# A conditioned two-MLP block: first slots counted on their own, conditioning bias by a matmul, late load of the last weights

## Chip, core and metric

The kernel runs on one core of a Trainium2 chip (trn2). The metric is the device time of one execution in microseconds (us), median of the runs. Engines are named as the profile names them: PE is TensorE (PEld its weight loads), DVE is VectorE, ACT is ScalarE, POOL is GpSimd, SP is SyncE, which here only issues transfers.

## What is computed

`x` is 32 sequences of 128 tokens with 512 features, `t` one conditioning vector of 512 per sequence, `mask` marks some tokens at the end of each sequence (up to 32 of 128). All is float32.

```python
emb = silu(t) @ ada_w + ada_b
shift, scale, gate_msa = split(emb, 3, axis=1)
norm = where(m, layernorm(x) * (1 + scale[:, None]) + shift[:, None], 0)
fwd = gelu(norm @ ssm_w1 + ssm_b1) @ ssm_w2 + ssm_b2
bwd = flip(gelu(flip(norm) @ bwd_w1 + bwd_b1) @ bwd_w2 + bwd_b2)
x = x + gate_msa[:, None] * where(m, fwd + bwd, 0)
ff_ada = silu(t) @ ffada_w + ffada_b
shift_mlp, scale_mlp, gate_mlp = split(ff_ada, 3, axis=1)
ff_norm = layernorm(x) * (1 + scale_mlp[:, None]) + shift_mlp[:, None]
return x + gate_mlp[:, None] * (gelu(ff_norm @ ff_w1 + ff_b1) @ ff_w2 + ff_b2)
```

The first MLP (both directions together, 512 to 1024 to 512) touches only the marked tokens. The second MLP (512 to 1024 to 512) touches all 4096.

## The kernel before

**Slots.** The marked tokens are packed into 512 slots, in four tiles of 128. Which token stands in a slot is counted on the chip. `pick_slots(h)` (L246) compares 256 slot numbers with the first and last slot of each sequence; `slots_to_count` (L254) multiplies the result with the running count of marked tokens, one small matmul for each tile of slots; `counted` (L261) turns that into token numbers on VectorE (compare, sum, add). The opening counts tiles 0 and 1 together (L567), and `gather` (L280) fetches their rows by two indirect transfers on POOL's queue. If more than 512 tokens are marked, a loop at the end (L1557) does the rest; with these inputs it has nothing to do.

**Transfers.** SP issues nearly all loads and stores, in the order of the program. `load_behind_gathers` (L138) writes one element of the destination on POOL first; so the load on SP waits until POOL has come past the gathers, and everything behind it on SP waits too. Each DMA counts up one of eight semaphores in turn, so an issue can also wait for a much older transfer.

**Conditioning.** `modulation_matmuls` (L299) forms `silu(t) @ ada_w` in four column strips of 32 batches, so that partition 32 j + b of `pm` holds block j of batch b. The bias is loaded for all 128 partitions (`load_conditioning_bias`, L129: three transfers of 64 KB for each of the two conditionings) and added by VectorE (`modulation_rows`, L311). `of_slots` (L315) spreads the rows to the slots ("strips"). Between the four groups of L609, and once behind the strips (L617), `keep_clock` (L596) runs matmuls whose result nobody reads, and `on_zeros` (L444) does the same on zeros.

**First MLP.** Tiles 0 and 1 are normalised, transposed (L192), multiplied with `w1` (L649, L201) and `w2` (`project`, L217), and finished by `finish_slots` (L362). Tiles 2 and 3 follow; `finish_late` (L1364) finishes them. Output banks of tiles 0, 1 and 2 begin with the bias (`seeded_with_bias`, L234); that of tile 3 gets it by an addition on VectorE (L1367).

**Second MLP.** It runs over four pairs (`p`) of two sides with four sequences each. Both of its products are made from seven block products, P1 to P7, in the manner of Strassen and Winograd. `FirstProduct` (L1003) does so on two levels: seven streams j, each with P1 to P7, in `window`s (L1185) of seven block products that end stream `old` and begin stream `new` (order 1, 2, 5, 6, 3, 7, 4). Streams 5, 6, 7 and 4 use sums of weights that were stored in DRAM (`t_rows`, L717) and are loaded for each pair by `load_weights` (L1037): block 1 for stream 5, 2 for 6, 3 for 7 (issued when stream 5 has ended, L1426), 4 for 4. `SecondProduct` (L1204) uses `fw2` and the three differences that `Weights.combine` (L383) makes of it: the first two stand in the opening (L1378), the others in the second product of the first pair. `token_sums` (L1015) and `TokenBlocks` (L946) make the sums of the token side on VectorE. `take_first_half` (L861) fetches the result rows of the first MLP into the tiles of a pair, by eight indirect transfers on POOL.

The order on each engine is written out by hand (the program is under a manual schedule until L1546): `fills` and `fill` hang steps behind a given product of a window or step.

Of the kernel before, what the change touches and what calls it, by code (L numbers as in the profile page):

```python
# [9 lines left out]
F32 = mybir.dt.float32  # L10
I32 = mybir.dt.int32
U8 = mybir.dt.uint8
BF16 = mybir.dt.bfloat16
AF = mybir.ActivationFunctionType
ALU = mybir.AluOpType
# [7 lines left out]
def kernel(  # L23
# [105 lines left out]
    def load_conditioning_bias(t, vec, kinds, queue):  # L129

        rows = vec.rearrange("(m j c) -> m j c", m=3, c=P)
        for m in kinds:
            queue.dma_start(t[:, m], rows[m].unsqueeze(1).to_broadcast([KC, B, P]))

# [7 lines left out]
    modb_a = adap.tile([P, 3, P], F32, tag="modb", name="modb_a", bufs=1)  # L142
# [8 lines left out]
    load_conditioning_bias(modb_a, ada_b, range(2), nc.sync)  # L151
# [94 lines left out]
    def pick_slots(h):  # L246

        part = ts(h, NH)
        nc.vector.tensor_scalar(inside[:, part], slot_row[:, part], behind, None, ALU.is_lt)
        nc.vector.scalar_tensor_tensor(  # L250
            pick[:, part], slot_row[:, part], first, inside[:, part], ALU.is_ge, ALU.mult
        )

    def slots_to_count(picked, n, name, bank):  # L254

        pl = bank[0].tile([P, 512], F32, tag=bank[1], name=f"pl_{name}")
        for c in range(n):
            nc.tensor.matmul(pl[:, ts(c, S)], picked[:B, ts(c, P)], rank, start=True, stop=True)
        return pl[:, : n * S].rearrange("p (c s) -> p c s", s=S)
# [38 lines left out]

    def modulation_matmuls(pm, ada, lo, hi, blocks):  # L299
        kinds = ada.rearrange("p k (m d) -> p k m d", d=D)  # L300
        for k in blocks:
            for j in range(KC):
                nc.tensor.matmul(
                    pm[ts(j, B), : (hi - lo) * P],
                    sT[:, k, :],
                    kinds[:, k, lo:hi, ts(j, P)],
                    start=(k == 0),
                    stop=(k == KC - 1),
                )

    def modulation_rows(pm, mod, modb, lo, hi):  # L311
        view = pm[:, : (hi - lo) * P].rearrange("p (m c) -> p m c", c=P)
        nc.vector.tensor_tensor(mod[:, lo:hi], view, modb[:, lo:hi], ALU.add)
# [130 lines left out]
    def on_zeros(*widths):  # L444
        for n in widths:
            nc.tensor.matmul(pm_keep_clock[:, :n], zeros[:, :P], zeros[:, :n], start=True, stop=True)
# [85 lines left out]
    pick_slots(0)  # L532

    nc.vector.tensor_scalar(rank[:, : S - 1], pg[:B, : S - 1], first[:B], None, ALU.add)

# [8 lines left out]
    on_zeros(256)  # L544
    nc.scalar.copy(sT.rearrange("p k b -> p (k b)"), ptr[:, : KC * B])
    warm = stp.tile([1, 1], F32, tag="warm", name="warm", bufs=1)
# [6 lines left out]
    load_conditioning_bias(modb_a, ada_b, (2,), nc.scalar)  # L553

    every = adap.tile([B, 3, P], BF16, name="every")
    nc.vector.memset(every, 1.0)
    for j, batches in ((1, 2 * G), (2, G)):
        nc.gpsimd.affine_select(
            out=every[:, j],
            in_=every[:, j],  # L560
            compare_op=ALU.is_gt,
            fill=0.0,
            base=batches,
            pattern=[[0, P]],
            channel_multiplier=-1,
        )
    token_i = tokens_of(pick[:, :NH], slot_col[:, : NC // 2], NC // 2, "s0", ssm)  # L567
    both = xp.tile([P, 2, D], F32, tag="x", name="xc_0")
    xc += [both[:, c] for c in range(2)]
    gather(xc[0], token_i[:, 0:1])  # L570
    load_behind_gathers(w1[:, :, :D], ssm_w1)
    gather(xc[1], token_i[:, 1:2])
# [15 lines left out]
    pick_slots(1)  # L588
# [4 lines left out]
    nc.vector.tensor_scalar(slot_of, slot_of, FAR, None, ALU.add)  # L593

# [13 lines left out]
    for k in range(KC):  # L608
        modulation_matmuls(pm, ada_a, 0, 2, (k,))  # L609
        if k < KC - 1:  # L610
            keep_clock(1, k)
    slots_of_late = slots_to_count(pick[:, NH:], NC // 2, "s1", (ps_h, "h"))
    nc.vector.tensor_scalar(modb_a[:, 1], modb_a[:, 1], 1.0, None, ALU.add)
    modulation_rows(pm, mod1, modb_a, 0, 2)

    strips = of_slots(pick, (0, 1), mod1, slice(0, 2), 3 * [(ps_o, "o")] + [(ps_h, "h")], "part_s0")
    keep_clock(1, 0)  # L617
# [26 lines left out]
    modb_f = adap.tile([P, 3, P], F32, tag="modb", name="modb_f", bufs=1)  # L644
    load_conditioning_bias(modb_f, ffada_b, range(3), nc.gpsimd)
# [31 lines left out]
    modulation_rows(pm, mod1, modb_a, 2, 3)  # L677
# [45 lines left out]
    for j in range(3):  # L723
        nc.tensor.matmul(pt[:, j : j + 1], every[:, j], count, start=True, stop=True)
# [33 lines left out]
    for n in range(2):  # L758
        own_statistics(raw[n], 2, f"x_{n}")
# [5 lines left out]
    for c in range(2):  # L765
        xn_late.append(
            modulated_by_strips(
                xc[2 + c], strips, c, spare[1][:, c], mv_t[:, c, 0:1], rstd_t[:, c : c + 1]
            )
        )  # L770
        if c == 0:
            nc.vector.tensor_tensor(b2, b2, b2b, ALU.add)
    h1 += hidden(xT_s, NH, w1, 0, AF.Gelu, "s0", ssm, range(KC, HC))
# [8 lines left out]
    store_rows = [finish_slots(0, project(0, h1, w2, "s0", seeded=po_s[0]), gs[0])]  # L782
    own_statistics(raw[3], 2, "x_3")
# [4 lines left out]
    nc.vector.tensor_scalar(modb_f[:, 1], modb_f[:, 1], 1.0, None, ALU.add)  # L788
# [22 lines left out]
    modulation_matmuls(pm, ada_f, 0, 3, range(KC))  # L811

# [19 lines left out]
    normalised_of_side_0(range(1))  # L832
    modulation_rows(pm, mod2, modb_f, 0, 3)
    normalised_of_side_0(range(1, 2))
# [510 lines left out]
    def load_of_pair_1():  # L1345
        nc.sync.dma_start(b2_row, b2[0:1, :])
        broadcast_rows(fb2, ff_b2, nc.sync)
        x_of[1] = [load_side(1, 0, spare), None]
# [7 lines left out]
        6: [turn_rows(3), lambda: load_behind_gathers(fw2, ff_w2), lambda: store_weight_sums(4, 1, 2)] + store_rows,  # L1356
        7: [load_of_pair_1],
# [6 lines left out]
    def finish_late(at, po, bias=None):  # L1364
        t = tp.tile([P, D], F32, tag="t", name=f"t_s_{at}")
        if bias is not None:
            nc.vector.tensor_tensor(t, po, bias, ALU.add)  # L1367
            po = t
        nc.vector.tensor_tensor(t, po, gs[at], ALU.mult)
        nc.vector.tensor_tensor(t, t, xc[at], ALU.add)  # L1370
        nc.sync.dma_start(x1_rows[ts(at, P), :], t)

    finish_late(2, project(0, h1, w2, "s2", {2 * k: turn(k) for k in range(KC)}, seeded=po_s[2]))
    po = project(1, h1, w2, "s3", bank=(ps_h, "h"))
# [3 lines left out]
    fw2_of.combine(0, 1)  # L1378
    for j in (3, 4):
        of_x[0].one(j)  # L1380
    finish_late(3, po, b2)
# [3 lines left out]
    now = FirstProduct(0, of_x[0].cut(), of_w)  # L1385
    now.load_weights(1)
    x_of[1][1] = load_side(1, 1)
    now.load_weights(2)
    for n in range(2):
        now.token_sums(1, n)  # L1390
# [6 lines left out]
    now.seed(2)  # L1397
    now.do(1, "P3")
# [3 lines left out]
    take_first_half(1, x_of[1])  # L1402
    for n in range(2, 4):
        now.token_sums(1, n)
# [5 lines left out]
    for p in range(NP):  # L1410
# [18 lines left out]
        if p == 0:  # L1429
            put(  # L1430
                5, 1, nc.vector.tensor_tensor,
                fb2_step, fb2[:, D // 2 :], fb2[:, : D // 2], ALU.subtract,
            )
        put(6, 0, now.late_gelu, "11")
# [233 lines left out]
```

## Time and profile before

| what | value |
|---|---|
| median of 3 runs (lowest, highest) | 457.67 us (457.63, 458.54) |
| the profiled execution | 457.94 us, of which its span is 456.2 us |
| PE busy in the span | 445.3 us |
| DVE, ACT, POOL busy | 332.8, 176.9, 161.2 us |
| transfers | 70.98 MB, mean 156 GB/s |
| `fw2` load: issued, landed | 70.44, 81.67 us |
| first gather: issued, landed after | 7.95 us, 4.6 us |

How to read the lines: in the timeline a line begins with the start and the busy time of a group in us, then the engine, the line of the kernel, the operation, its output and inputs by tile name, the shape and the count; what stands in brackets is the idle time of the engine just before and what ended it. A float32 matmul of the program is two entries of the trace. In a group line ("| busy, mean ns |") the mean is that of one entry. A line of windows gives the stretch, its length, the busy time (and instructions) of PE, PEld, DVE, ACT and POOL, the granted clock, the share of the DMA engines and the GB/s. Waits for several semaphores are put down to the one that came last.

### The profile page before, as it was taken

To read this page: it belongs to the slowest core of one execution; us is meant where nothing else is said; L and a number is where in the kernel's file an instruction comes from. 1 tells how busy PE (TensorE), PEld (TensorE's weight loads), DVE (VectorE), ACT (ScalarE), POOL (GpSimd) and SP (SyncE) were. 2 spreads that over 40 slices of the span, in tenths; PEclk is the share of its full clock that TensorE was granted. 3 is DMA by queue.
4 is the path that set the end of the run, shared out by engine and by line. 5 is a ranking of instruction groups with operands and counts; after the bars stand their busy time and mean duration, and the time that the engine had idled before them with its cause. 6 is when DMAs were issued, how large, how long until landed. Compare 5 with 4: busy or idle time off the path is not lost.

```text
span 456.2 us, 6196 instructions
## 1 busy us (share of the span) xinstructions
PE 445.3 (98%) x2161; PEld 370.9 (81%) x2161; DVE 332.8 (73%) x570; ACT 176.9 (39%) x387; POOL 161.2 (35%) x155
## 2 busy tenths in 40 slices
PE   8999999979999999999999999999999999999995
PEld 4784485668888888888888888888888888888884
DVE  4797887978779749895796398867963995534645
ACT  3123126244543551545435515454355154552000
POOL 4230560079770000697700006977000027560000
PEclk9999999999999999999999999999999999999999
DMA  7999549982208725822187258221772442222022
GB/s 233 382 352 403 232 70 261 339 343 96 80 22 221 115 60 203 290 96 82 34 214 106 64 198 293 94 84 43 201 111 62 152 149 82 80 92 94 0 93 96
DMA packets 83201, 70.98 MB, mean 156 GB/s; under 512 B 63292, under 2 KB 64268, under 8 KB 82142
## 3 DMA queue, kind: packets, MB, share of 16 engines
q1 hardware_dynamic: 67994, 58.41, 41.0%
q0 software_dynamic: 4400, 10.74, 7.0%
q10 hardware_dynamic: 10772, 1.39, 2.2%
q8 instruction: 19, 0.31, 0.3%
q14 instruction: 16, 0.13, 0.1%
HBM read 56.84 MB, written 13.70 MB: 155 GB/s over the span
## 4 chain that ended last, share of the span: by engine, by line
PE 80%; DMA 13%; DVE 4%; SPq 1%; issue 1%; POOL 0%; ACT 0%; POOLq 0%; ACTq 0%; DVEq 0%
PE a_o L1283 23%; PE a_m L1096 20%; PE e_o L1283 18%; PE e_m L1096 15%; DMA fw<-in_L_cond_ff_w_dram 7%; DMA tw<-t_rows 2%; DMA w<-in_L_cond_ssm_w_dram 1%; PE ph_s L207 1%; DVE t L387 1%; DMA xT<-xn 1%; DMA x_wide<-t_s 1%; PE last L1283 1%; SPq L935 1%; DMA x<-x_wide,slot_i 1%; DVE fw L387 0%
## 5 line engine op out<-in xcount | busy, mean ns | idle before, releaser
L1147 POOL TENSOR_TENSOR ha<-p_m,ha 128x512 f32<-128x512 f32 x20 | 25.8, 1289 | 176.8 <-ACT ha L1154 167.4
L1283 PE MATMUL e_o<-fw,ha 128*128 128x256 f32 x256 | 57.9, 379 | 0.0
L918 ACT ACTIVATE xT<-xT,modT 128x128 f32<-128x128 f32 x112 | 44.0, 480 | 33.0 <-DMA xT<-xn 32.1
L1283 PE MATMUL a_o<-t,hb 128*128 128x256 f32 x240 | 54.1, 379 | 0.0
L1283 PEld LDWEIGHTS e_o<-fw,ha 128*128 128x128 f32 x256 | 48.7, 190 | 6.5
L1283 PEld LDWEIGHTS a_o<-t,hb 128*128 128x128 f32 x240 | 45.7, 190 | 6.1
L1058 ACT ACTIVATE hb<-hb,biasT 128x256 f32<-128x256 f32 x64 | 29.0, 500 | 27.9 <-POOL hb L1180 19.4
L1110 ACT COPY p_m<-e_m 128x512 f32<-128x512 f32 x27 | 15.8, 585 | 50.1 <-PE e_m L1096 50.1
L864 POOL DMA_INDIRECT x<-x_rows,slot_i x24 | 28.5, 1186 | 6.8 <-issue 4.9
L224 PE MATMUL po_s<-w,h_s 128*128 128x512 f32 x64 | 28.7, 596 | 0.9 <-DMA w<-in_L_cond_bwd_w_dram 0.9
L1147 POOL TENSOR_TENSOR hb<-p_m,hb 128x512 f32<-128x512 f32 x20 | 29.4, 1470 | 0.3
L1283 PE MATMUL a_o<-t,s 128*128 128x256 f32 x128 | 28.9, 380 | 0.0
L1283 PE MATMUL a_o<-fw,ha 128*128 128x256 f32 x128 | 28.9, 379 | 0.0
L1283 PE MATMUL e_o<-fw,s 128*128 128x256 f32 x128 | 28.9, 379 | 0.0
L1154 ACT COPY ha<-e_m 128x512 f32<-128x512 f32 x32 | 18.5, 579 | 25.2 <-PE e_m L1096 24.7
L1283 PEld LDWEIGHTS a_o<-t,s 128*128 128x128 f32 x128 | 24.4, 190 | 3.2
L1283 PEld LDWEIGHTS a_o<-fw,ha 128*128 128x128 f32 x128 | 24.4, 190 | 3.3
L1283 PEld LDWEIGHTS e_o<-fw,s 128*128 128x128 f32 x128 | 24.4, 190 | 3.2
L1121 DVE TENSOR_TENSOR e_m<-a_m,ha 128x512 f32<-128x512 f32 x20 | 13.9, 697 | 16.7 <-POOL ha L1147 6.6
L1058 ACT ACTIVATE ha<-e_m,biasT 128x256 f32<-128x256 f32 x48 | 20.0, 467 | 14.7 <-PE e_m L1096 12.5
L1096 PE MATMUL a_m<-xT,tw 128*128 128x256 f32 x96 | 24.7, 380 | 0.0
L1126 DVE TENSOR_TENSOR hb<-a_m,hb 128x512 f32<-128x512 f32 x20 | 13.7, 685 | 15.0 <-PE a_m L1096 15.0
(235 smaller groups left out, 904.5 us busy)
## 6 DMA issues: line engine op xcount, KB each, us to landing
tw<-t_rows SPq DMA_DIRECT2D x16, 896.0 KB, 5.5
x<-in_x_dram SPq DMA_DIRECT2D x16, 512.0 KB, 12.0
gate<-gate_rows POOLq DMA_DIRECT2D x8, 1024.0 KB, 5.2
out_dram<-x SPq DMA_DIRECT2D x15, 512.0 KB, 4.4
xT<-xn SPq DMA_DIRECT2D x92, 64.0 KB, 2.4
fw<-in_L_cond_ff_w_dram SPq DMA_DIRECT2D x2, 2048.0 KB
ada_f<-in_L_cond_ffada_w_dram SPq DMA_DIRECT2D x4, 768.0 KB, 13.9
ada_a<-in_L_cond_ada_w_dram SPq DMA_DIRECT2D x4, 512.0 KB, 5.3
```

The source lines that it names most:

```text
L207: nc.tensor.matmul(ph[:, :n], w[:, k, ts(f, P)], xT[:, k, :], start=(k == 0), stop=(k == KC - 1))
L224: nc.tensor.matmul(po, h[f][:, ts(i, P)], w[:, f, :], start=(f == 0 and seeded is None), stop=(f == HC - 1), skip_group_check=seeded is no ...
L864: nc.gpsimd.indirect_dma_start(out=xs[i // G][i % G // 2][:, i % 2], out_offset=None, in_=x1_rows, in_offset=bass.IndirectOffsetOnAxis(ap= ...
L918: nc.scalar.activation(out, src, AF.Identity, bias=shift, scale=scale)
L1058: nc.scalar.activation(dst[:, n], src[:, n], AF.Gelu_apprx_tanh, bias=biasT[:, f : f + 1])
L1096: nc.tensor.matmul(bank[:, ts(n, QT)], self.w_block(j, product)[:, ts(n, P)], self.x_block(j, product), start=(product in ("P1", "P5") and ...
L1110: nc.scalar.copy(p5, e)
L1121: nc.vector.tensor_tensor(e, a, p5, add)
L1126: nc.vector.tensor_tensor(dst, a, dst if prior else self.p5[j], add)
L1147: nc.gpsimd.tensor_tensor(self.place(RESULT[j], c), self.p5[j], other, ALU.add)
L1154: nc.scalar.copy(self.place(RESULT[j], c), src)
L1283: nc.tensor.matmul(part, src[:, k, ts(i, P)], w[product][:, k, :], start=(last and k == 0), stop=True, skip_group_check=True,)
```

## The change

1. Slots: `pick_slots` takes a slice; the first 128 slots are picked before `rank`, the second 128 after it. The two count matmuls of tiles 0 and 1 have an `on_zeros` between them, and each tile is counted on VectorE and gathered for itself. The `every` tile has 3 instead of 384 columns, is made behind the gathers by POOL and is spread by a stride of zero as matmul weights.
2. Conditioning bias: both bias vectors are loaded as 4 rows each (one transfer on SP ahead of `ada_w`, one on ACT ahead of the silu). A matmul with four rows (`quarter`, made from the identity by two ScalarE copies) adds them to `pm`; VectorE then only copies. The "+ 1" of the scale works on the four rows. The six 64 KB transfers are gone, and so are the filler groups between the four groups of the first conditioning; behind the strips stand four filler groups instead of one.
3. `fw2` is loaded in the first pair, behind its eight gathers and the second `load_weights`; its first two differences move from the opening to windows 5 and 6.
4. Smaller moves: the bank of tile 3 is seeded with the bias like the others, and `finish_late(3)` stands before the third and fourth token block; the stores of tiles 2 and 3 are issued before `load_weights(1)`; the statistics of `raw[1]` come after the modulation of tiles 2 and 3; the second conditioning's rows are taken before the first normalised row; the first two token sums stand behind `seed(2)`; the `b2_row` store is issued earlier.

```diff
-    modb_a = adap.tile([P, 3, P], F32, tag="modb", name="modb_a", bufs=1)
+    modb = adap.tile([B + KC, 3, P], F32, name="modb")
+    AT_A, AT_F = slice(0, KC), slice(B, B + KC)
+    for queue, at, vec in ((nc.sync, AT_A, ada_b), (nc.scalar, AT_F, ffada_b)):
+        queue.dma_start(modb[at], vec.rearrange("(m j c) -> j m c", m=3, c=P))
...
-    load_conditioning_bias(modb_a, ada_b, range(2), nc.sync)
...
+    def modulation_bias(pm, at, lo, hi):
+        nc.tensor.matmul(
+            pm[:, : (hi - lo) * P],
+            quarter[at],
+            modb[at, lo:hi],
+            start=False,
+            stop=True,
+            skip_group_check=True,
+        )
...
-        nc.vector.tensor_tensor(mod[:, lo:hi], view, modb[:, lo:hi], ALU.add)
+        nc.vector.tensor_copy(mod[:, lo:hi], view)
...
-    pick_slots(0)
+    pick_slots(ts(0, P))
 
     nc.vector.tensor_scalar(rank[:, : S - 1], pg[:B, : S - 1], first[:B], None, ALU.add)
+    pick_slots(ts(1, P))
...
+    slots_of_first = slots_to_count(pick, NC // 2, "s0", (ps_t, "tr"), lambda: on_zeros(256))
+    token_i = [
+        counted(slots_of_first[:, c : c + 1], slot_col[:, c : c + 1], 1, f"s0_{c}", ssm)
+        for c in range(2)
+    ]
...
-    for k in range(KC):
-        modulation_matmuls(pm, ada_a, 0, 2, (k,))
-        if k < KC - 1:
-            keep_clock(1, k)
+    modulation_matmuls(pm, ada_a, 0, 2, range(KC))
+    modulation_bias(pm, AT_A, 0, 2)
     slots_of_late = slots_to_count(pick[:, NH:], NC // 2, "s1", (ps_h, "h"))
...
-    keep_clock(1, 0)
+    keep_clock(4, 0)
...
-    modb_f = adap.tile([P, 3, P], F32, tag="modb", name="modb_f", bufs=1)
-    load_conditioning_bias(modb_f, ffada_b, range(3), nc.gpsimd)
...
+    po_s.append(seeded_with_bias(3))
...
-        6: [turn_rows(3), lambda: load_behind_gathers(fw2, ff_w2), lambda: store_weight_sums(4, 1, 2)] + store_rows,
+        6: [turn_rows(3), lambda: store_weight_sums(4, 1, 2)] + store_rows[:2],
...
-    po = project(1, h1, w2, "s3", bank=(ps_h, "h"))
+    po = project(1, h1, w2, "s3", seeded=po_s[3])
     of_x[0] = TokenBlocks(0, xT)
     for j in (1, 2):
         of_x[0].one(j)
-    fw2_of.combine(0, 1)
+    finish_late(3, po)
     for j in (3, 4):
         of_x[0].one(j)
-    finish_late(3, po, b2)
...
+    for g in store_rows[2:]:
+        g()
     now.load_weights(1)
-    x_of[1][1] = load_side(1, 1)
+    x_of[1].append(load_side(1, 1))
     now.load_weights(2)
-    for n in range(2):
-        now.token_sums(1, n)
...
     take_first_half(1, x_of[1])
+    load_behind_gathers(fw2, ff_w2)
...
+            put(5, 6, fw2_of.combine, 0)
+            put(6, 3, fw2_of.combine, 1)
```

## Prediction

> **What bounds the kernel now.** I read the page first, then TensorE's timeline with the wait before each group, then the chain of waits, then the queues behind the waits found.
>
> ```profile
> span 456.2 us, 6196 instructions
> PE 445.3 (98%) x2161; PEld 370.9 (81%) x2161; DVE 332.8 (73%) x570; ACT 176.9 (39%) x387; POOL 161.2 (35%) x155
> ...
> PE a_o L1283 23%; PE a_m L1096 20%; PE e_o L1283 18%; PE e_m L1096 15%; DMA fw<-in_L_cond_ff_w_dram 7%; DMA tw<-t_rows 2%; DMA w<-in_L_cond_ssm_w_dram 1%; PE ph_s L207 1%; DVE t L387 1%; DMA xT<-xn 1%; DMA x_wide<-t_s 1%; PE last L1283 1%; SPq L935 1%; DMA x<-x_wide,slot_i 1%; DVE fw L387 0%
> ```
>
> TensorE is busy for 98%. In order of time the chain changes hands until 97 us, and from there on it is matmuls to the end. So the time is TensorE's work plus its gaps in the first 100 us. These are the gaps after its start:
>
> ```profile
> 40.13 10.57 PE L224 MATMUL po_s<-w,h_s 128*128 128x512 f32 x24 [0.94 <-DMA w<-in_L_cond_bwd_w_dram]
> ...
> 56.60 0.44 PE L845 MATMUL ptr_mod<-ident,mod 128*128 128x128 f32 x2 [0.39 <-DVE mod L313]
> ...
> 90.44 1.13 PE L1096 MATMUL e_m<-s,fw 128*128 128x256 f32 x4 [0.64 <-DVE e_m L1121]
> ...
> 97.33 1.10 PE L1096 MATMUL e_m<-sx,tw 128*128 128x256 f32 x4 [2.30 <-DMA tw<-t_rows]
> ```
>
> Start to start, one product takes 0.865 (84.45, 85.32, 86.18). At that pace the last two gaps cost 0.8 (88.77 + 0.865 = 89.6 against 90.44) and 2.5 (94.00 + 0.865 = 94.9 against 97.33). With 0.94 and 0.39 all four make 4.6 us: no edit outside the opening can gain more. The profiled execution took 457.94, 1.74 more than its span; the median of the runs shown is 457.67.
>
> **The change, part by part.** All times are of the trace before.
>
> *First gather.* `pick_slots` on 128 columns takes, by the 256-column rows (0.35 and 0.48) less half of their streaming, about 0.25 and 0.33, so `rank` ends 0.25 earlier. One count matmul (two of them took 1.12) and the three VectorE steps on one tile (0.82 instead of 1.07) bring the token at about 6.5 instead of 7.65. The gather goes out at 6.9 instead of 7.95, and w1, which SP sends behind it at 9.32, at 8.2. The gather landed 4.6 us after its issue, so its tile is there at 11.5 or a little before, no longer at 12.55.
>
> *Conditioning.* Three filler groups of 0.855 leave the start. But TensorE runs at half speed there:
>
> ```profile
> L303 PE MATMUL pm_ss<-ada_a,sT 128*32 128x256 f32 x8 | 1.1, 635 | 0.0
> ...
> L303 PE MATMUL pm_ss<-ada_a,sT 128*32 128x256 f32 x8 | 0.6, 380 | 0.0
> ```
>
> The first answer is of 6.4 to 7.3, the second of 11.5 to 12.1: 635 ns became 380 ns at about 11.3, although the page's clock row shows full speed throughout. Four groups from 6.4, unfilled, end at 9.8 if `ada_a` is there (2.1 MB in one piece from 2.4 at the 400 GB/s of 3 to 5 us: 8.2; so it is). The bias matmul has four rows but streams 256 columns: 0.43 warm by half of a product's 0.865, 0.86 here. Then the late counts (0.63 warm, 1.12 cold), the strips (1.07), the fillers now four groups instead of one (0.43 to 0.53 each, so 1.9), the two fillers on `xn` (1.05):
>
> ```profile
> 13.74 0.64 PE L599 MATMUL pm_keep_clock<-ada_a,sT 128*32 128x256 f32 x8
> 14.49 1.22 PE L629 MATMUL pm_keep_clock<-xn_s,ident 128*128 128x256 f32 x4
> 15.54 0.83 PE L196 MATMUL ptr_s<-ident,xn_s 128*128 128x128 f32 x4
> ```
>
> 9.8 + 0.86 + 1.1 + 1.07 + 1.9 + 1.05 = 15.8 against 15.54. VectorE could have had `xn` at 14.7 (statistics at 11.3 instead of 12.61, then the same 3.4), but TensorE comes to the transposes only behind its fillers: the earlier gather buys nothing, +0.2. What bounds it: without the fillers in the way 14.8, −0.7; with late speed below, +2.
>
> Here the Trainium skill, "TensorE: Matmul & The Clock Gate", Part 1, speaks against the edit: half speed is the default, full speed comes after a busy window of about 3.4 us that runs freely. By the row, dense tiles had run from 6.4 for 4.9 us. After the change they run densely from 6.4 to 9.8 only, then comes a four-row matmul and small counts. If that window does not count as busy, full speed comes one window later, at 14.7: the strips and fillers up to there cost double and the transposes come at about 17.3. The rest of the sum takes the same 11.3; this goes into a rival.
>
> The other two bias matmuls lie on TensorE's path with nothing beside it: 128 columns 0.25, 384 columns 0.65. The VectorE adds become copies (0.42, 0.29, 0.52 as before, no gain).
>
> *DMA up to 40 us.* w1 and all behind it start 1.1 earlier; six 64 KB broadcasts (0.39 MB) go, 0.26 MB of them in the saturated part, 0.65 us at 390 GB/s. The w2 half that ended the 0.94 gap lands near 38.3. TensorE is there at 39.2 + 0.2 + 0.25 = 39.65: gap gone, −0.5. fw1 comes about 1.8 earlier, but `finish_slots` waits for projections that end at 43.6 and 50.5, so side 0 moves by 0.3 only. mod2 is now taken ahead of the first row, so the 0.39 gap goes. At 84.45 TensorE stands at −0.5 + 0.65 − 0.4 = −0.25.
>
> *Edits at nothing.* The statistics of `raw[1]` (1.74) move into VectorE's 3.12 idle ahead of 37.41; without that idle they would hold fw1's sums by 1.74. The two "+ 1" steps lie in its 2.81 idle before `mod`, the `quarter` copies in ScalarE's 9.7 before 16.41, `every` behind the gathers in POOL's 3.3 before 13.79, the fourth seeded bank in ScalarE's 12.7 before 51.17, the `b2_row` store on SP between 47.8 and 50.6. The feed-forward bias, issued on ScalarE's queue ahead of the silu (0.4), delays that by 0.25 of the 0.9 that it has until 4.27. If all these covers were gone, some 0.5 us; they aren't.
>
> *First product.* fw2's 2.1 MB, sent at 70.44, leave SP's queue (5 us at 420 GB/s), and two sums of 1.23 leave VectorE. `finish_late(3)`, one step of 0.7 shorter, now stands ahead of token blocks 3 and 4 and waits for the projection's end (84.2): 84.4 to 85.8, blocks until 88.2. The product that waited at 90.44 needs `e_m`, ready by 89.6: gap 0.1. The bank of the second P1 is now freed by `finish_late(3)`: 0.1. The weight sums, sent at 89.10 behind the two row stores, go at 86.4 with little ahead of them: 1.5 + 0.5/0.42 + 0.92/0.42 gives 91.5, needed at 94.4. The 2.5 go. TensorE: −0.25 − 0.8 − 2.5 + 0.2 = −3.35.
>
> *Where fw2 goes.* It waits for POOL's marker behind eight gathers, and on SP it stands ahead of the third weight block.
>
> ```profile
> 95.88 1.11 POOL L864 DMA_INDIRECT x<-x_rows,slot_i  x1 [0.66 <-DMA tw<-t_rows]
> ...
> 106.93 1.00 POOL L864 DMA_INDIRECT x<-x_rows,slot_i  x1 [0.30 <-issue]
> ...
> 110.00:112.00 2.00, 2.00 (x11) 1.77 (x10) 1.40 (x4) 0.86 (x2) 2.00 (x3) 1.00 0.61 147
> 112.00:114.00 2.00, 2.00 (x11) 1.77 (x10) 1.27 (x3) 0.58 (x1) 2.00 (x2) 1.00 0.75 316
> ...
> 115.53 1.03 PE L1096 MATMUL e_m<-s,tw 128*128 128x256 f32 x4
> ```
>
> Before, that block left at 109.7, moved its 0.92 MB from 111.3 to 113.5 (last column, GB/s) and was read at 115.53: 2 us to spare. After, the gathers follow `with_p5` (its input is there 0.9 earlier, and they no longer wait 0.66 for a transfer), so 94.2, and take the eight times 1.49 of before (busy 1.19 and 0.30): until 106.1. fw2 leaves at 106.2, the block right behind its issue at 106.6 (its own release is at 109.7 − 3.35). "DMA: Bandwidth & Descriptors", Queues, rings and completion order, says descriptors of one ring are consumed in order. By it the block lands at 106.2 + 1.6 + 5.0 + 2.2 = 115.0; by the row for the block alone, at 110.6; TensorE wants it at 115.53 − 3.35 = 112.2. Between 0 and 2.8 us; I take 2.8, since the 8.1 us of the load at 89.10 fit a queue emptied in order. So 2.8 of the 3.35 come back as a new wait; queued behind fw2 on SP are this block and the fourth (before at 115.7, wanted 6 us later: not late). fw2 itself lands at 113, needed by VectorE's moved sums at 122; these (2 x 1.23) fit into idle 0.67 and 1.03 and delay seeds to within 0.2 of their reader: 0.
>
> Sum: −3.35 + 2.8 = −0.55, for span and median alike (the 1.74 around the span stay): 457.67 − 0.5 = 457.2. The gathers hang on TensorE's own position, so the opening's error goes through in full.
>
> **Rivals.**
> 1. *New wait behind fw2* (above): 457.2, own range 456.3 to 458.0. For it: order on SP, and 3.0 MB in 6 us. Chance 0.47.
> 2. *The block is not held up* (gathers quicker, or both transfers share): −3.35, 454.3. For it: 2 us to spare and an idle queue at 105 to 109; against it: SP's order. Chance 0.23.
> 3. *Full speed one window later.* Place: strips and the four filler groups; price half a us for each us that the switch comes after 11.3, 1.5 in all, hence 458.7; the sum turns slower than before from a switch at about 12.4. For it: TensorE matmuls from 1.26 had not brought full speed by 7.9. Against: no idle time up to 11.3. Chance 0.25.
> 4. *The gaps at 40 and 90 stay* because transfers don't move: +0.94 + 0.8 on case 1, 458.9. Chance 0.05.
>
> **How the numbers follow.** A measurement tells about 0.2% (0.9 us) from no change. Case 2 is faster (0.23); case 1 lies mostly within, with 0.12 below and 0.05 above; case 3 is slower for 0.17, case 4 for 0.05. Faster 0.35, same 0.38, slower 0.27. Predicted 457.2; range 454.0 (case 2 and a little) to 459.1 (case 3 and a little).
>
> **What would show it.** Right: transposes of the first tile at 15.5 to 16.0 with no wait; no gap at 40; mod2 without a gap; the first weight-sum product at about 94 without a wait; a wait of 2 to 3 us on `tw` at the first product of stream 7, near 112. Wrong: no such wait (case 2); 635 ns matmuls after 12 us (case 3); a wait for w2 or fw1 still there (case 4).

## The result, and the profile after

The changed kernel takes 470.93 us (median of 4 runs, 467.57 to 473.03) against 458.03 us for the kernel before on the same chip (457.63 to 458.54). The ratio is 1.027, with a 95% interval of 1.020 to 1.034: slower by 12.9 us, where 0.5 us faster was predicted, and outside the range. The profiled execution took 472.46 us with a span of 470.7, which is 14.5 above the 456.2 of before. The four executions lie 5.5 us apart, those of before 0.9; that spread is itself a part of the answer, and the one profiled is the second longest. A ratio leaves out runs of over 1.5% above the fastest of their kernel and is not the quotient of two medians.

First the page after, then TensorE's waits (engine, line, what it waited for; us in all, times, longest):

```profile
PE 454.7 (97%) x2167; PEld 373.1 (79%) x2167; DVE 334.2 (71%) x573; ACT 178.1 (38%) x390; POOL 160.8 (34%) x153
```

```profile
PE e_m L1113 <- DMA tw<-t_rows: 4.7, 1, 4.7
PE e_m L1113 <- DVE e_m L1157: 1.8, 3, 0.8
...
PE a_o L1300 <- ACT a_o L1239: 0.5, 1, 0.5
PE pm_ss L310 <- DMA ada_a<-in_L_cond_ada_w_dram: 0.4, 2, 0.2
```

TensorE is busy for 9.4 us more, although the change takes filler work away: busy time grows where the same matmuls run at half speed. The waits of before on `w`, on mod2 and on the first `tw` block are gone, as predicted; four others stand in their place. I laid the two timelines of TensorE beside each other, matmul by matmul. The start of the same instruction, before and after:

| point on TensorE | before | after | shift |
|---|---|---|---|
| transposes of the first tile | 15.54 | 19.70 | +4.16 |
| first product | 84.45 | 87.53 | +3.08 |
| stream 7, without its wait | 115.53 | 118.74 | +3.21 |
| stream 7, with its wait | 115.53 | 123.44 | +7.91 |
| first a_o product of the second MLP | 127.62 | 137.95 | +10.33 |
| second pair, before its first wait | 168.19 | 179.28 | +11.09 |
| second pair, behind its last wait | 200.14 | 214.50 | +14.36 |

So there are four places: the opening (3.1 left at 84), the wait at stream 7 (4.7), slow matmuls behind that wait (2.4), and the way into the second pair (0.75 + 3.3). The first product itself, from its first matmul to stream 7, was to win over 3 us and won nothing (+0.13).

*The opening.* TensorE's timeline after (start, busy time, then as before):

```profile
8.97 1.08 PE L310 MATMUL pm_ss<-ada_a,sT 128*32 128x256 f32 x8 [0.23 <-DMA ada_a<-in_L_cond_ada_w_dram]
10.21 1.08 PE L310 MATMUL pm_ss<-ada_a,sT 128*32 128x256 f32 x8 [0.16 <-DMA ada_a<-in_L_cond_ada_w_dram]
...
14.97 3.64 PE L617 MATMUL pm_keep_clock<-ada_a,sT 128*32 128x256 f32 x32
...
19.70 0.60 PE L192 MATMUL ptr_s<-ident,xn_s 128*128 128x128 f32 x4
```

Eight entries take 1.08 throughout, where before they took 0.61 from 11.5 on. The four filler groups alone cost 3.64. The wait for the last part of `ada_a` ended at 10.21, not by 8.2.

*The wait.* SP's queue, then TensorE:

```profile
111.42 0.37 SPq L130 DMA_DIRECT2D fw<-in_L_cond_ff_w_dram  x1
111.89 7.22 SPq L1059 DMA_DIRECT2D tw<-t_rows  x2
```

```profile
117.71 1.03 PE L1113 MATMUL a_m<-xn_sy,tw 128*128 128x256 f32 x4
123.44 2.05 PE L1113 MATMUL e_m<-s,tw 128*128 128x256 f32 x4 [4.70 <-DMA tw<-t_rows]
125.28 1.91 PE L1113 MATMUL a_m<-xT,tw 128*128 128x256 f32 x4
```

The block leaves 0.47 behind fw2 and lands at 123.30, 11.4 after its issue; TensorE had been ready at 118.74. The same four entries take 1.03 before the wait and 2.05 and 1.91 behind it. The windows show the granted clock (third figure from the right) at 0.50 from 122 to 128, and how slowly the transfers begin (last figure, GB/s):

```profile
112.00:114.00 2.00, 1.99 (x10) 1.44 (x9) 1.29 (x2) 0.91 (x2) 2.00 (x3) 1.00 0.67 172
114.00:116.00 2.00, 1.55 (x8) 1.04 (x7) 1.05 (x3) 0.59 (x1) 2.00 (x2) 1.00 0.88 290
...
120.00:122.00 2.00, 0.00 (x0) 0.00 (x0) 0.85 (x3) 0.00 (x0) 1.26 (x1) 0.84 1.02 386
122.00:124.00 2.00, 0.56 (x2) 0.50 (x2) 0.00 (x0) 0.00 (x0) 0.00 (x0) 0.50 0.80 337
...
126.00:128.00 2.00, 2.00 (x6) 1.56 (x6) 0.70 (x2) 0.16 (x1) 1.69 (x2) 0.50 0.00 0
```

*The way into the second pair.* The largest of its waits after, and the same two matmuls before:

```profile
198.68 1.13 PE L1113 MATMUL e_m<-xT,fw 128*128 128x256 f32 x4 [0.53 <-DVE e_m L1157]
...
211.80 1.13 PE L1113 MATMUL e_m<-xn_sy,tw 128*128 128x256 f32 x4 [0.77 <-DVE e_m L1157]
```

```profile
185.46 1.03 PE L1096 MATMUL e_m<-xT,fw 128*128 128x256 f32 x4
...
197.55 1.03 PE L1096 MATMUL e_m<-xn_sy,tw 128*128 128x256 f32 x4
```

### The profile page after: what moved, and what is told of

Its sections match the earlier page's. It is cut to its first block, busy times and chain, and to the rows that moved or that the text cites. A ratio compares the mean times of both kernels' runs of the same rounds, so it can differ in the third digit from the quotient of the medians.

```text
span 470.7 us, 6202 instructions
## 1 busy us (share of the span) xinstructions
PE 454.7 (97%) x2167; PEld 373.1 (79%) x2167; DVE 334.2 (71%) x573; ACT 178.1 (38%) x390; POOL 160.8 (34%) x153
## 4 chain that ended last, share of the span: by engine, by line
PE 76%; DVE 8%; DMA 5%; SPq 4%; issue 3%; ACT 3%; POOL 2%; DVEq 0%; ACTq 0%; POOLq 0%
PE a_o L1300 17%; PE a_m L1113 15%; PE e_o L1300 13%; PE e_m L1113 12%; PE po_s L220 6%; PE ph_s L203 4%; SPq L952 3%; DMA tw<-t_rows 2%; PE ph_s L669 2%; DMA ada_a<-in_L_cond_ada_w_dram 2%; DVE sx L1042 1%; ACT xT L935 1%; PE pm_keep_clock L617 1%; PE last L1300 1%; DMA xT<-xn 1%
## 5 line engine op out<-in xcount | busy, mean ns | idle before, releaser
L1075 ACT ACTIVATE hb<-hb,biasT 128x256 f32<-128x256 f32 x64 | 29.0, 500 | 29.7 <-POOL hb L1197 19.7
L1127 ACT COPY p_m<-e_m 128x512 f32<-128x512 f32 x27 | 15.8, 585 | 52.1 <-PE e_m L1113 51.8
L220 PE MATMUL po_s<-w,h_s 128*128 128x512 f32 x64 | 28.4, 594 | 0.0
L1113 PE MATMUL e_m<-s,fw 128*128 128x256 f32 x92 | 24.6, 391 | 0.4 <-DVE s L982 0.3
```

The costliest lines, as they stand in the source:

```text
L220: nc.tensor.matmul(po, h[f][:, ts(i, P)], w[:, f, :], start=(f == 0 and seeded is None), stop=(f == HC - 1), skip_group_check=seeded is no ...
L1075: nc.scalar.activation(dst[:, n], src[:, n], AF.Gelu_apprx_tanh, bias=biasT[:, f : f + 1])
L1113: nc.tensor.matmul(bank[:, ts(n, QT)], self.w_block(j, product)[:, ts(n, P)], self.x_block(j, product), start=(product in ("P1", "P5") and ...
L1127: nc.scalar.copy(p5, e)
```

## Experiments

Each is an edit to the changed kernel unless it says otherwise. The times are medians; the ratio is to the kernel before, with its 95% interval. A number "of the trace" is of one execution.

**Whose wait is it? fw2 behind the third block (e1).**

```diff
-    load_behind_gathers(fw2, ff_w2)
     for n in range(2, 4):
...
         put(3, 6, now.load_weights, 3)
+        if p == 0:
+            put(3, 6, load_behind_gathers, fw2, ff_w2)
```

> The changed kernel with one edit: the load of fw2 is issued behind the third weight block in SP's order, not ahead of it. Theory A (the block waits behind fw2's 2 MB, and TensorE then also loses its clock): the wait of 4.70 us for tw at the start of stream 7 is gone, no half clock follows it (another 2.4 us), so the profiled run is about 7 us shorter than the changed kernel's 472.5: 464 to 466. Rival (the queue is simply full, and the wait moves to the fourth block or to the gathered rows): a wait of 3 us or more on tw at the start of stream 4, and 469 to 472. The opening keeps its 4 us: first transposes near 19.7.

465.85 us, 1.0163 (1.0146 to 1.018). The wait at stream 7 is gone, and a wait of 2.6 on tw stands at stream 4: the fourth block now leaves behind fw2 (114.91 and 118.53). Theory and rival both hold a part: the block behind fw2 waits, whichever it is. But the 5.1 us are not this edit's doing alone: of the 6.4 between the two profiled executions some 4 lie in the way into the second pair, whose waits this one doesn't show.

**The fillers back (e2), and both (e3).** In e2 the fillers stand as before: one group behind each of the first three conditioning groups, one behind the strips.

```diff
-    modulation_matmuls(pm, ada_a, 0, 2, range(KC))
+    for k in range(KC):
+        modulation_matmuls(pm, ada_a, 0, 2, (k,))
+        if k < KC - 1:
+            keep_clock(1, k)
     modulation_bias(pm, AT_A, 0, 2)
...
-    keep_clock(4, 0)
+    keep_clock(1, 0)
```

> The changed kernel with the fillers of before in the opening: one group of filler matmuls behind each group of conditioning matmuls, and one instead of four behind the strips. Theory A (short waits for ada_a between the conditioning groups keep TensorE at half speed until 18 us): no gap from 6 us on, matmuls of 128x256 at full speed from about 11.5 to 12.5, first transposes near 16 instead of 19.7, and 3 to 4 us off the changed kernel's time: 468.5 to 469.5. Rival (full speed comes late for another reason, such as the one filler fewer before the counts): half speed to 17 or later, transposes near 18, 470.5 to 472.5. The wait of 4.7 us at stream 7 stays in both.

467.76 us, 1.0194 (1.0142 to 1.0245): 3.2 less in the median, though the four runs (465.25 to 470.05) overlap those of the changed kernel. Full speed comes at about 12.2, the transposes start at 16.63, the wait at stream 7 is 4.6.

```profile
10.99 1.08 PE L617 MATMUL pm_keep_clock<-ada_a,sT 128*32 128x256 f32 x8
11.84 0.77 PE L310 MATMUL pm_ss<-ada_a,sT 128*32 128x256 f32 x8
```

> The changed kernel with both edits: fw2 behind the third block, and the fillers back. If the two causes are independent, their gains add: 472.5 - 7 - 3.5 = about 462; if the small waits of the second pair (3.3 us between 183 and 212) come from the late start they go too, and it is 457 to 459. Rival (the small waits have a cause of their own, the handover of the next pair's turned tiles): 461 to 463.

463.98 us, 1.0142 (1.0111 to 1.0172). The gains of e1 and e2 (5.1 and 3.2) make 7.0 together; with e2's spread, whether they add is not settled.

**Is the slow stretch the idle time's doing? Ten matmuls ahead of stream 7 (e4).**

```diff
+            if self.p == 0 and new == 7:
+                self.pad(7, 10)
```

> The changed kernel with ten extra matmuls (ident by fb2, 0.43 us each, written to the bank that stream 7 clears) placed ahead of stream 7, so that TensorE works while tw is on its way; the result is unchanged. Theory A (the half clock from 122 to 128 follows from the idle 4.7 us): the matmuls behind the wait run at 379 ns, and the time falls by 2 to 2.5 us, to about 470. Rival (the half clock comes from something else, such as power or the DMA traffic): matmuls at over 600 ns stay, and the time is 472 to 473.

464.04 us, 1.0141 (1.0113 to 1.0169). TensorE at stream 7:

```profile
114.68 4.48 PE L1206 MATMUL e_m<-fb,ident 128*128 128x256 f32 x20
119.40 1.13 PE L1113 MATMUL e_m<-s,tw 128*128 128x256 f32 x4 [0.24 <-DMA tw<-t_rows]
```

The transfer is as late as ever, but the matmuls behind it keep 1.03. From stream 7 to the first a_o product it is 12.19 (119.40 to 131.59), in the changed kernel 14.51: 2.3 us of half clock, theory A. But 7 us went in the median, and 9.3 between the two profiled executions. The rest is in two places that the edit did not touch: the way into the second pair, where this execution has lost only 0.75 of the 4.0, and the opening (3.9). That is, instruction for instruction, the changed kernel's:

```profile
10.12 0.64 PE L310 MATMUL pm_ss<-ada_a,sT 128*32 128x256 f32 x8 [0.22 <-DMA ada_a<-in_L_cond_ada_w_dram]
...
12.98 1.93 PE L617 MATMUL pm_keep_clock<-ada_a,sT 128*32 128x256 f32 x32
...
15.81 0.60 PE L192 MATMUL ptr_s<-ident,xn_s 128*128 128x128 f32 x4
```

Here full speed came at 9.7, with the same two waits on `ada_a`; the first product starts at 83.63, 0.8 ahead of before. So the changed opening is a draw of lots: 9.7 in this execution, 19.0 in the one profiled of the changed kernel and 18.6 in e1's.

**fw2 behind the last block (e5), and there with the token sums early (e8).**

> The kernel of e3 (fillers back) with fw2 issued behind the fourth weight block, the last that the first product reads. Theory A (whichever block is queued behind fw2's 2 MB is late): no wait on tw anywhere, no half clock after 20 us, and e3's 2.7 us wait with some 1.5 us of half clock behind it are gone: 459.5 to 460.5. Rival (fw2 now lands too late for its own combine): a wait of 2 us or more ahead of the first product of fw2 (near 128), and 462 to 464.

465.82 us, 1.0171 (1.0134 to 1.0207): the rival, and more than it gave. VectorE waits for fw2, TensorE for VectorE, and TensorE is then at half clock until 134.0:

```profile
127.05 1.43 DVE L395 TENSOR_TENSOR t<-fw 128x1024 f32<-128x1024 f32 x1 [4.59 <-DMA fw<-in_L_cond_ff_w_dram]
```

```profile
129.14 2.07 PE L1116 MATMUL e_m<-xT,tw 128*128 128x256 f32 x4 [4.23 <-DVE e_m L1160]
```

The combine stands in VectorE's order ahead of the product's own `e_m`. fw2 left at 118.15 and landed 8.9 us later, 4.6 after VectorE was ready for it. Of the three places tried in this stretch (changed kernel, e1, e5) none has room for its 2 MB.

> The kernel of e5 with the first two token sums back ahead of the first product, where the kernel before had them, instead of behind P6 of stream 1. Theory A (the sums stand in VectorE's order ahead of what TensorE waits for): the waits for VectorE between 94 and 116 (3.1 us in all in the changed kernel) shrink to under 1, and about 0.8 comes back at the fourth product: e5 minus 1.5 to 2.5, 457 to 459. Rival (VectorE is short of time in this stretch wherever the sums stand): e5's time within 0.5 us.

464.42 us, 1.0142 (1.0106 to 1.0178): 1.4 under e5. The two waits for `hb` (0.6 and 0.2) go, one of 0.3 comes at 89, and those at 103 to 111 stay.

**fw2's move undone: with the fillers (e6), without (e11).** Load and first two combines stand where the kernel before has them; all else of the change stays.

> The changed kernel with the fillers back and the whole move of fw2 undone: its load stands where the kernel before had it, and its first two combines too. Theory A: no block waits behind fw2, 459.5 to 461; the token sums behind P6 still cost their small VectorE waits, 3 us between stream 2 and stream 7. Rival (the gap of 2.5 us at the start of stream 5 in the kernel before was fw2's doing): it comes back beside the VectorE waits, and the time is 462 to 463.

458.46 us, 0.9999 (0.9973 to 1.0025): the kernel before, and better than theory and rival had it. TensorE waits 1.43 for `e_m` at 91.67 and 0.69 for tw at 96.95, nowhere else in this stretch.

> The changed kernel with only the move of fw2 undone (its load and first two combines where the kernel before had them); the opening stays as the change has it, without the fillers. Theory A (the opening costs up to 4 us, in some executions, by the clock alone): e6's 458.5 plus 0 to 4, a median of 459.5 to 461.5 and a spread of 3 us or more, with no wait on tw of over 1 us and no half clock after 25 us. Rival (the opening costs nothing by itself): within 0.5 us of e6.

460.66 us (456.94 to 464.82 in 22 runs), 1.0036 (1.0013 to 1.0059). fw2's move, load and combines, is thus 10.3 of the 12.9 us. In the execution profiled, full speed came at 10.0 and the span is 455.6, below that of before: a lucky opening is 1.3 us ahead at 84 us, an unlucky one 3 behind.

**The fillers alone, taken out of the kernel before (e7).**

> The kernel before with one edit: the three groups of filler matmuls between the conditioning groups are left out. Theory A (the waits for ada_a that the fillers cover keep TensorE from full speed, in some executions and not in others): two short waits on ada_a near 8.5 and 10, 635 ns matmuls to 15 us or later in many executions, times spread over 457 to 462. Rival (the fillers cover nothing that counts): full speed near 11 in every execution, and 456.5 to 458, within 0.3% of the kernel before.

459.49 us (457.87 to 466.54 in 22 runs), 1.0028 (1.0012 to 1.0045): 0.1 to 0.5% worse, with executions up to 8 us longer. Two waits on `ada_a`, 2.4 us together, full speed at 17.6, transposes at 18.06 instead of 15.54.

**What decides the moment of full speed? Short bridges (e13), zeros of full length (e16).** Both on e11: one 128x512 product of zeros behind groups two and three, or two behind each of the first three.

> The kernel of e11 (fw2's move undone, no fillers in the opening) with one short filler (one 128x512 product of zeros in bf16) behind the second and one behind the third conditioning group, where TensorE waited for ada_a. Theory A (it is the short idle times on ada_a that put off full speed): the two waits are gone from the trace, and the executions draw together: a median of 457.3 to 458.3 and a spread like that of e6, against e11's 460.66 and 457 to 465. Rival (it takes fillers of some length, or the moment is chance): a median of 459.5 to 461 and a spread over 5 us.

460.76 us, 1.0047 (1.0026 to 1.0067). No wait on `ada_a` is left, and yet:

```profile
10.17 0.61 PE L454 MATMUL pm_keep_clock<-zeros 128*128 128x512 bf16 x1
...
15.47 3.64 PE L617 MATMUL pm_keep_clock<-ada_a,sT 128*32 128x256 f32 x32
```

Half speed to 19.1. The idle times on `ada_a` alone are not what decides; my theory fell.

> The kernel of e11 with fillers of the old length but another kind: two 128x512 products of zeros in bf16 (0.86 us together at half speed) behind each of the first three conditioning groups. Theory B (the unbroken stretch of full-height products ahead of the strips must be long enough: 5.7 us with the old fillers, 4 to 5 without): full speed before 13 us in the trace, and e6's time and spread, 457.5 to 459 in nine executions of ten. Rival (it takes the fp32 products on ada_a, or chance): half speed to 15 or later in the trace or in many executions, median 460 to 461.

461.45 us (459.43 to 464.61), 1.0064 (1.0044 to 1.0083). Full speed at 9.9 in the trace, but the runs do not draw together as hoped, and the zeros cost their own time.

*What the traces say of the lot.* Each trace keeps the clock's own record: the moments from which it was granted at full or at half. With the old fillers full came between 9.4 and 12.6 in all twelve traces (before's among them); without them at 9.7 to 10.2 in four and at 17.6 to 19.1 in four. In all twenty, the changes of the clock within a trace lie whole multiples of 3.41 us apart (changed kernel: full from 18.97, half from 121.37, full from 128.20). So the clock changes on a grid of 3.41 us, and where the grid lies differs from execution to execution: that is the lot. In the changed kernel two of its points were 8.73 and 12.15. The window between them holds two conditioning groups, each behind a wait for `ada_a`, and then the four-row bias matmul; full speed came two windows later. In e2, the same opening but for the fillers, the points were 8.76 and 12.17; that window is filled with groups, and full speed came at its end. In e4 they were 6.32 and 9.73, a window that three groups fill for the most part. That the old fillers narrow the draw is shown, and for one position of the grid also how: they fill a window that holds only two groups without them. How full a window has to be, and which products count, is open: e13's window from 8.84 to 12.26 had products of 128 rows for its first 2.9 us, two of its groups and the zeros, and full speed did not come.

**The late combines alone (e9), with the sums early (e10), with the block moved (e14, e15).** e9 is e6 with the two combines left late.

> The changed kernel with the fillers back and fw2 loaded where the kernel before loaded it, but its first two combines left late, as the change has them. Theory A (VectorE sets the pace between 84 and 116: the combines' 2.4 us moved out of it are worth their own time there only as far as the waits behind the token sums allow): the wait of 1.4 us at 91.7 that e6 showed is gone, the small waits between 94 and 116 are back (3 us), no wait on tw over 1 us; a wait of 0.5 us near 141 where the late combines stand; 458 to 459, e6's time within 0.3%. Rival (the late combines are a gain): 456 to 457.

461.46 us, 1.0066 (1.0049 to 1.0084): 3.0 over e6, more than either theory gave, and 6.3 under e2. With the fillers, then, the load's place costs about 6 us and the late combines 3. The wait of 0.5 for ScalarE is back (138.39), and all those of the second pair from 173 to 202.

> The kernel of e9 with the first two token sums back ahead of the first product. Theory A (e8 against e5: the place of the sums is worth 0.7 to 1.4 us): 457 to 458, that is the kernel before or up to 0.3% better. Rival (the 2.5 us gap at stream 5's start, a wait on tw, comes back as soon as VectorE is faster): e9's time or 0.5 above it.

460.54 us, 1.0039 (1.0023 to 1.0055): 0.9 less, with overlapping intervals, and a wait of 2.2 on tw at stream 5, the gap of before.

> The kernel of e6 (fillers back, fw2's move undone) with the first weight block issued ahead of the last two stores of the gathered rows in SP's order. Theory A (the wait on tw at the start of stream 5 comes from the block's place behind those stores): the wait of 0.7 us there is gone, and 0.5 to 0.9 us of time: 457.5 to 458. Rival (the block waits for room or for the rows of sums): the wait stays, and the time is e6's 458.5 within 0.3.

458.76 us, 1.0026 (1.0005 to 1.0046). The wait on tw is gone and the time is e6's: waits for VectorE of 0.3 and 0.6 came at 106 and 113. VectorE, busy for 27.3 of the 32 us from 84 to 116, sets the pace there as soon as `tw` doesn't.

> Both: the short bridges of e13 and the block of e14, on the changed kernel with fw2's move undone. If both hold, the opening is about 1.1 us shorter than with the fillers and the wait on tw is gone: 456.3 to 457.3, faster than both kernels by 0.2 to 0.4%. If the bridges do not hold the clock: 459 to 461.

462.07 us, 1.0073 (1.0037 to 1.011): no gain. Of the bridges its trace says nothing: full speed came early, at 10.2, and 3.3 us went in the second pair.

**The second pair: its turn on two queues (e17).** Between the pairs SP issues 28 DMAs that turn the next pair's tiles. Of e9, with a quarter of the first side on ScalarE's queue:

```diff
-            to_feature_rows(0, nc.sync)
+            to_feature_rows(0, nc.sync, nc.sync, nc.scalar)
```

> The kernel of e9 (late combines, two of three executions near 461 to 463) with 4 of the 16 DMAs that turn the next pair's first side moved from SP's to ScalarE's queue. Theory C (the small waits of the second pair come from SP's turn of 28 DMAs, which grows from 20.4 to 22 us when one of them takes over 2 us): the turn is 2.7 us shorter on SP, the waits between 172 and 202 are gone, and the executions near 461 to 463 with them: a median of 458 to 459. Rival (ScalarE's own work is then late): a new wait for ScalarE between 138 and 150, and 460 to 462.

459.19 us, 1.0001 (0.9974 to 1.0028), 2.3 under e9; none of the waits from 172 to 202. SP after, one piece of the chain of waits of the same execution, and SP in e17:

```profile
150.76 21.81 SPq L952 DMA_DIRECT2D xT<-xn  x28
```

```profile
154.01 2.32 SPq L952
```

```profile
141.48 20.53 SPq L955 DMA_DIRECT2D xT<-xn  x24
```

Before, the turn took 20.37. Seven traces (after, e2, e9, e10, e12, e13, e15) have one issue of 1.8 to 2.9 us in it, and all seven show the second pair's waits; of the other kernels only e16 shows two of them (0.5 and 0.8; it loses 1.8 us there, the seven 2.9 to 3.4). From SP's first issue to VectorE's first sum of the next pair's tiles it is 28.4 us before, 31.2 after, 31.3 in e9, 29.7 in e16 and 28.5 in e17. In e17 no issue takes over 1.3 us. But its turn is not 2.7 us shorter, as I had expected: the second side waits 2.5 us for transfers of the first. The place is shown, then, and that a quarter less on SP's queue takes the loss away; the late combines bring the two gate loads to 2.1 us from each other, and of the seven kernels where they stand so, five have the long issue, of the other thirteen two (e13, e15). So they make it likely and are not its only cause; why an issue takes 2 us is open.

**The first counts in a tile each (e12), on e10.**

> The kernel of e10 with the two first counts in a bank (tile) each, so that VectorE's first comparison waits for the first count alone. Theory A (the first gather was held by the second count, which shared its bank): the first comparison starts near 5.9 instead of 7.0 and the first gather is issued near 7.0 instead of 8.1; the time does not move, within 0.5 us of e10, because the strips, not the gathered rows, come last. Rival (the comparison waits for something else): the gather stays at 8.1.

462.03 us, 1.0082 (1.0061 to 1.0103). VectorE in the changed kernel, then POOL in e12:

```profile
6.98 0.29 DVE L261 TENSOR_TENSOR before_s<-pl_s,slot_col 128x127 f32<-128x127 f32 x1 [1.48 <-PE pl_s L255]
```

```profile
6.91 1.19 POOL L278 DMA_INDIRECT xc<-in_x_dram,token_i_s  x1 [3.79 <-DVE token_i_s L270]
```

The first comparison read one half of a tile that a second matmul was still to write, and waited for both; with two tiles it starts at 5.81 and the gather leaves at 6.91. But TensorE's second count then waits 0.66 for the first token, which suggests that both tiles took the same bank one after the other. The time is 1.5 above e10, not level with it; the trace has full speed at 12.6 against e10's 9.9, but that is one draw each, and why the median rose is not shown.

**The best parts together (e18):** e14 with the turn of e17.

> The parts that the runs speak for, together: the changed kernel with the fillers back, fw2's move undone, the first weight block ahead of the last stores (e14) and the turn on two queues (e17). Theory C: e14's executions near 461 to 463 (8 of 22) go, as e9's did in e17, and those near 457 to 459 stay: a median of 457.2 to 458.2, level with the kernel before or up to 0.2% faster. Rival (the spread has another source besides SP's turn): 458.5 to 459.5.

458.97 us, 1.001 (0.999 to 1.0031). Its slowest execution is 460.41 (e14: 462.96), which fits the turn as the source of the upper group; but there is no gain over the kernel before. No version of the change that was run beats that.

## Why the prediction was wrong

*What failed, by the sum's own terms.* Four steps did. The opening was taken to be ready for full speed: `ada_a` "there" at 8.2, the late clock a rival of 1.5 us. The first product's gain of 3.1 was reckoned without what would be waited for next. The transfer of `fw2` was sized at 6.6 us and took 9.7, and that idle time also slows the clock was not in the sum. The moved combines were put at nothing after a look at their next reader alone. Predicted −0.55, measured +14.5 in the profiled executions, where the opening and the second pair drew badly:

| term | predicted | measured |
|---|---|---|
| TensorE at 84.45 (opening, bias, gaps at 40 and 56) | −0.25 | +3.08 |
| first product, gaps at 90 and 97 against new ones | −3.1 | +0.13 |
| wait behind fw2 | +2.8 | +4.7 |
| slow clock behind that wait | not in the sum | +2.4 |
| moved combines, way into the second pair | 0 | +4.0 |

The rest, 0.14, lies behind 214.

*Conditioning.* "so it is" there at 8.2 was the step that failed: by its own numbers 2.4 + 2.1/0.4 is 7.65, and TensorE waited for the last part of `ada_a` until 10.21. The rival on full speed was given a quarter and 1.5 us. Its mechanism is real, and in e4, e11, e15 and e16 it did not strike. Where it struck, its price per microsecond held and its moment did not: full speed at 18.97 instead of 14.7, at half a us for each us after 11.3, makes 3.8, and 15.8 + 3.8 = 19.6 is where the transposes started (19.70). The filler groups that the change puts there ran cold (3.64 instead of 1.93). That the transposes of e4 start at 15.81, the predicted 15.8, is luck: conditioning ended 0.9 us later, and the bias and the counts, already at full speed, took 0.8 less. The window of about 3.4 us that the Trainium skill gives in "TensorE: Matmul & The Clock Gate", Part 1, free-running and to be busy for full speed, is the grid of 3.41 found here, and neither from 5.32 to 8.73 nor from 8.73 to 12.15 had the changed kernel more than two conditioning groups. But in e13 TensorE ran without a pause from 6.0 to 19.1, at half speed all the way, so the rule does not say which work counts.

*First gather.* At 8.08, not 6.9: the shared tile (e12). That it buys nothing was right.

*DMA up to 40 us, the bias matmuls, the edits at nothing.* Right: no gap at 40 or 56, and with a quick opening TensorE is at 83.63 (e4) and 83.18 (e11), better than the −0.25 that was worked out. e6 confirms them as a whole (0.9999); none was tried alone.

*First product.* Both gaps went (3.46 start to start, with the small ones). In their place came 3.41, nearly all put down to VectorE: 0.75 at 97.4, 0.38 at 104.0, 0.30 at 108.8, 0.62 at 115.9, and bits. (The table's +0.13 has 0.17 of the wait behind it, because a matmul starts that long before the one ahead of it ends.) For the weight sums 86.4 + 1.5 + 1.2 + 2.2 is 91.3, not 91.5; nothing hangs on it. I had priced VectorE's sums at the one product that they held up, and not the stretch as a whole: the token sums now stand behind P6, in front of other results that TensorE reads. e8, e10 and e14 show that taking one wait away there brings the next.

*Where fw2 goes.* The mechanism of the likeliest case was right and its size off. A transfer counts up its semaphore sixteen times as it lands. By these counts fw2 had landed at 121.15, the block behind it at 123.30, and the fourth, issued at 118.8, at 125.48: in the order of issue, as the prediction took it. (By the same counts the block of before landed at 114.61, 0.9 and not 2 us ahead of its reader.) The block lands 2.15 behind fw2 (2.1 to 2.2 in e1 to e4 as well; 2.2 predicted). The term that was too small is fw2's own: 9.7 us from issue to landing, and 8.9 to 10.0 in the seven kernels that load it late, instead of 1.6 + 5.0. It moved at 172 GB/s in the first two us, 290 in the next and 380 only then, not at 420 throughout; why it starts slowly is open. That is 3.1 us. TensorE came to the block 7.2 us after fw2's issue instead of 6.0, which gives 1.2 back: 2.8 + 3.1 − 1.2 = 4.7. That idle time costs twice, by the clock, was not in the sum; e4 shows it at 2.3.

*Moved combines.* "fit into idle" held for TensorE, the next reader, only to 0.5 us (e9: 138.39). What was missing is the reader after that: VectorE's tiles for the next pair, SP's turn of 20 us behind them, ScalarE, and VectorE again. That handover had little slack; e4 with its late combines lost 0.75 there, e3 0.3 and e1 nothing.

## What to carry to other kernels

A bulk load that is moved "later" needs a place with room on both sides: here whatever stood behind it in its queue was late, and one place further on its own reader was. Price an idle TensorE at the wait plus a slow stretch behind it, and count filler matmuls as what holds the clock before taking them for dead work. Where two timelines are compared, look at the start of the same instruction along the whole run: a shift that grows far behind the edit points to a handover without slack.

## Not expected of the hardware

Short idle times can halve the clock. In e9 TensorE, with 0.58 and 1.05 us idle inside 3 us:

```profile
96.26 1.79 PE L1116 MATMUL e_m<-sx,tw 128*128 128x256 f32 x4 [1.05 <-DMA tw<-t_rows]
97.84 1.91 PE L1116 MATMUL a_m<-sx,tw 128*128 128x256 f32 x4
```

By the clock's record TensorE was at half for 3.4 us there, for 3.4 in e1 (2.6 idle), for 3.4 in e17 (0.6 and 1.5 idle) and for 6.8 in the changed kernel (4.7 idle); 2.3 us idle in the kernel before and 2.2 in e10 cost nothing. The lengths are one and two of the windows of about 3.4 us that "TensorE: Matmul & The Clock Gate", Part 1, tells of; but that it takes an idle window of that length to lose the clock does not hold here, and the measurement decides. Where the idle time falls on the grid has a part in it: in e10 the 2.2 us lay on both sides of a point (95.18), in e1 the 2.6 inside one window. It is not the whole rule: the window that kept its clock before had 1.8 us idle in it, the one that lost it in e9 only 1.6.

In the opening the windows give the granted clock as 1.00 while 128x256 entries take 635 ns, because the record begins only where full speed does: there the first entry of the record or the duration of the matmuls tells.
